# Order of the score products, the place of the norms' variance, and the order of a key copy in an attention and mixture-of-experts kernel

## The chip, the cores and the metric

The kernel runs on one core of a Trainium2 chip. The metric is the device time of one execution in microseconds. Three executions of the kernel before took 4326.62, 4331.74 and 4331.98 us, a median of 4331.74. One more execution was profiled: 4321.7 us, of which the profile's span covers 4319.9.

## The reference, cut to what matters

The input is `x`, float32, 2 images of 128 channels by 256 x 256 pixels. One layer is computed:

- A layer norm over the channels of each pixel, then three 1x1 convolutions to q, k, v (128 channels each, 4 heads of 32).
- Attention in windows of 8 x 8 queries over 12 x 12 keys around them, with relative position logits and a fixed mask. The mask leaves to each query only the keys at an even distance in both directions, so that the pixels fall into 4 independent planes (even or odd row, even or odd column). In one plane a window has 4 x 4 queries and 6 x 6 keys.
- The softmax, the product with v, an output convolution, and a residual sum.
- A layer norm over the channels of each pixel again, a router with 8 experts of which the best 2 are kept, 8 expert matrices of 128 x 128, the gated sum and a second residual sum.

```python
x = x + conv_attention(ln_c(x), W_qkv, W_out, rel_height, rel_width)
t = to_tokens(x)
t = t + moe(ln_t(t), router_w, router_b, expert_w, expert_b)   # softmax, top 2 of 8
```

## The kernel before, in words

**Tiling.** An image is cut into strips of 8 rows (`R = 8`), 32 per image and 64 in all. A strip has 4 planes, so that there are 256 planes, numbered `n`; `i, pl = divmod(n, 4)` gives strip and plane. The main loop makes one turn for each `n`, and 7 more to finish. One turn holds, woven together, the attention of plane `n`, the projections of plane `n + 1`, the norms of a row pair, the routing of an earlier row pair, and the 8 expert products of a still earlier one.

**What a plane's attention does.** A plane of a strip has 4 rows of 128 columns: 512 queries in 32 windows of 16. The windows are taken in pairs, so that 60 keys (6 rows by 10 columns, padded to `SLOT = 64`) serve 32 queries. There are 16 pairs. `kcol` (4 buffers) holds the keys column by column: in a pair's 64 places, the row is the inner index (stride 1) and the column the outer one (stride 6). Scores stand in PSUM transposed: keys on the partitions, queries along the free axis. 8 pairs use partitions 0 to 63 of the tile `att` (`half` 0), the other 8 partitions 64 to 127 (`half` 1), and each head has a PSUM bank of its own.

- `scores` (line 462) first puts the position logits into `att` (line 474, 16 products with 128 queries each), then adds the products of keys and queries (line 491). These are 64 products: for each `t` of 8, each `half` of 2 and each head `h` of 4, one with 32 rows (the channels of a head, on partitions 32 h to 32 h + 31), 64 columns (the keys) and 32 queries. The row group that a product uses in TensorE's array is set by the head, the column half by `half`. The trace shows two matmul and two weight-load records for each float32 product, 128 of each for line 491 in a plane. An exponential on ScalarE follows (line 499).
- `attend` (line 503) sums the weights over the keys (line 512) and multiplies with v (line 522): again 64 products, with 64 rows (a half), 32 columns (a head) and 32 queries. VectorE then forms `o` (lines 532 to 542), and `out_project` multiplies with the output matrix (line 550) and adds the residual (line 555).
- `project` (line 400) makes the next plane's v rows (line 350), position projections (409), keys (423) and queries (445). The new keys go from PSUM into `kcol` with two ScalarE copies for each run of rows: line 434 for the 14 inner pairs, line 441 for the two at the ends. A run has 4 rows in two of every three strips, and two runs of 2 rows stand in the third.

**Norms.** `norms` (line 563) makes the statistics of two row pairs in one tile `plt` on TensorE (line 580), and VectorE transposes them into `plg`, a PSUM tile of 512 columns of which the first 128 are used (line 589). `rstd` (line 222) takes mean and mean square from `plg` and computes variance, plus epsilon, and its inverse root, on 4 to 8 columns: copy (232), square (233), variance (234), floor and epsilon (235) on VectorE, logarithm and exponential on ScalarE (236, 237), a Newton step on VectorE (238, 239, 596, 598). The tiles `u` (variance) and `r` are in SBUF, and so is `epsc`, the table of the two epsilons. `route` and `spread` use the result in the next turn.

**What sets the order.** The main loop runs under a manual schedule: every engine executes its instructions in the order in which the loop issues them. The engines meet only at semaphores. VectorE makes 6 of the 8 gated inputs of the experts (line 705), GpSimd the other 2; GpSimd is held back by a small copy (`last`, line 709) until VectorE has made its last one, then multiplies one, makes a row of `xn` (line 276), in one turn of four copies a halo row (line 250), and multiplies the second. SyncE's queue issues all DMAs of the loop in order. Before the scores of each plane from `n = 6` on, line 823 (`addr_align`) puts fillers into TensorE's instruction stream, so that it lies at a fixed place in a block of 256 instructions; the trace shows 31 NOP records in each steady turn, right after TensorE's wait for `o` and over 2.2 us.

## Time and profile before

| | |
|---|---|
| median of three executions | 4331.74 us |
| profiled execution: time, span | 4321.7 us, 4319.9 us |
| TensorE matmul, busy | 4217.3 us, 98% of the span |
| TensorE weight load, busy | 2466.8 us, 57% |
| VectorE, busy | 3852.5 us, 89% |
| ScalarE, busy | 1452.8 us, 34% |
| GpSimd, busy | 1086.0 us, 25% |
| granted TensorE clock, mean | 0.992 |
| DMA: mean rate | 237 GB/s |

A row of a profile gives an engine, a line of the kernel, the operation, output and inputs with partitions by elements, and a count; in lists of groups the busy time and the mean of one follow, and the idle time just before them with what ended it. In lists in order of time the first column is the start in us, the second the time taken. Matmul records overlap: a busy TensorE is not a TensorE at its peak, so that the time of a stage is read from start to start. Where a wait is put down to "issue", the engine waited for nothing that the profile shows.

### The profile page before, as it was taken

To read this page: it belongs to the slowest core of one execution; us is meant where nothing else is said; L and a number is where in the kernel's file an instruction comes from. 1 tells how busy PE (TensorE), PEld (TensorE's weight loads), DVE (VectorE), ACT (ScalarE), POOL (GpSimd) and SP (SyncE) were. 2 spreads that over 40 slices of the span, in tenths; PEclk is the share of its full clock that TensorE was granted. 3 is DMA by queue.
4 is the path that set the end of the run, shared out by engine and by line. 5 is a ranking of instruction groups with operands and counts; after the bars stand their busy time and mean duration, and the time that the engine had idled before them with its cause. 6 is when DMAs were issued, how large, how long until landed. Compare 5 with 4: busy or idle time off the path is not lost. (4 is left out here: it accounts for less than half of the span.)

```text
span 4319.9 us, 224653 instructions
## 1 busy us (share of the span) xinstructions
PE 4217.3 (98%) x94273; PEld 2466.8 (57%) x94273; DVE 3852.5 (89%) x11850; ACT 1452.8 (34%) x3774; POOL 1086.0 (25%) x1126
## 2 busy tenths in 40 slices
PE   7899999999999999999999999999999999999987
PEld 4455555555555555555555555555555555555553
DVE  4799999999999999999999999999999999999977
ACT  3333333333333333333333333333333333333321
POOL 1222222222222222222222222222222222222211
PEclk9999999999999999999999999999999999999999
DMA  3678777787777777778787777777778787877765
GB/s 109 209 236 247 240 247 242 241 246 242 245 242 244 247 240 248 243 239 247 241 248 240 246 243 243 245 242 246 241 243 244 240 250 238 247 247 241 243 193 191
DMA packets 824580, 1022.19 MB, mean 237 GB/s; under 512 B 137634, under 2 KB 409634, under 8 KB 823594
## 3 DMA queue, kind: packets, MB, share of 16 engines
q1 hardware_dynamic: 822864, 1007.52, 75.4%
q8 instruction: 769, 12.60, 1.3%
q14 instruction: 217, 1.78, 0.1%
q10 hardware_dynamic: 730, 0.29, 0.0%
HBM read 863.78 MB, written 143.75 MB: 233 GB/s over the span
## 5 line engine op out<-in xcount | busy, mean ns | idle before, releaser
L714 PE MATMUL acc<-xe,ew 128*128 128x512 f32 x4096 | 1915.4, 600 | 18.6 <-DVE gb L688 16.5
L714 PEld LDWEIGHTS acc<-xe,ew 128*128 128x128 f32 x4096 | 758.1, 190 | 936.6 <-issue 886.5
L705 DVE TENSOR_TENSOR xe<-xs,gb 128x512 f32<-128x512 f32 x1536 | 950.6, 686 | 11.1 <-DMA gb<-gd 1.1
L709 POOL COPY last<-xe 128x1 f32<-128x1 f32 x256 | 47.1, 184 | 3113.7 <-DVE gb L688 3107.2
L705 POOL TENSOR_TENSOR xe<-xs,gb 128x512 f32<-128x512 f32 x512 | 650.6, 1272 | 1.5 <-PE att L522 0.7
L491 PE MATMUL att<-qs,kcol 32*64 32x32 f32 x32768 | 400.6, 226 | 11.1 <-issue 10.8
L434 ACT COPY kcol<-pk 128x560 f32<-128x560 f32 (+2 forms) x344 | 318.8, 927 | 275.3 <-PE pk L423 272.5
L491 PEld LDWEIGHTS att<-qs,kcol 32*64 32x64 f32 x32768 | 396.7, 131 | 13.9 <-issue 13.6
L276 POOL TENSOR_TENSOR xn<-xt,rb 128x512 f32<-128x512 f32 x249 | 373.7, 1501 | 91.1 <-DMA rb<-gd 74.6
L522 PEld LDWEIGHTS att<-pT,vwin 64*32 64x32 f32 x32768 | 348.6, 105 | 40.8 <-issue 3.2
L522 PE MATMUL att<-pT,vwin 64*32 64x32 f32 x32768 | 345.1, 200 | 2.4 <-issue 2.2
L499 ACT ACTIVATE pT<-att 128x1024 f32<-128x1024 f32 x256 | 261.9, 1023 | 180.3 <-PE att L491 180.1
L350 PE MATMUL pv<-wt,xn 128*128 128x128 f32 x2048 | 301.1, 291 | 0.9 <-issue 0.9
L574 ACT ACTIVATE sq<-xt 128x512 f32<-128x512 f32 x505 | 291.8, 629 | 0.0
L397 DVE STREAM_TRANSPOSE au<-auT 128x512 f32<-128x512 f32 x256 | 272.1, 1063 | 9.0
L550 PE MATMUL po<-o,wt 128*128 128x512 f32 x512 | 264.9, 599 | 9.5 <-DVE o L542 5.9
L409 PE MATMUL pu<-xn,wrel 128*128 128x512 f32 x512 | 266.2, 602 | 1.2 <-issue 1.2
L445 PE MATMUL pq<-xn,wt 128*128 128x512 f32 x512 | 261.9, 592 | 0.9 <-issue 0.8
L423 PE MATMUL pk<-xn,wt 128*128 128x512 f32 (+2 forms) x528 | 261.4, 578 | 0.0
L350 PEld LDWEIGHTS pv<-wt,xn 128*128 128x128 f32 x2048 | 251.7, 193 | 11.8 <-issue 1.3
L474 PEld LDWEIGHTS att<-au,keys 32*64 32x64 f32 x8192 | 118.9, 132 | 234.0 <-PE po L550 181.1
L413 DVE STREAM_TRANSPOSE uT<-pu 128x512 f32<-128x512 f32 x256 | 177.1, 692 | 65.5 <-PE pu L409 63.6
(2696 smaller groups left out, 4946.0 us busy)
## 6 DMA issues: line engine op xcount, KB each, us to landing
gb<-gd SPq DMA_DIRECT2D x2048, 256.0 KB, 5.5
vwin<-vrows SPq DMA_DIRECT2D x512, 240.0 KB, 5.1
xt<-in_x_dram SPq DMA_DIRECT2D x256, 256.0 KB, 6.5
sb<-gd SPq DMA_DIRECT2D x256, 256.0 KB, 4.1
out_dram<-xt SPq DMA_DIRECT2D x256, 256.0 KB, 6.0
rb<-gd SPq DMA_DIRECT2D x249, 256.0 KB, 3.4
vrows<-vr SPq DMA_DIRECT2D x168, 256.0 KB, 3.8
vrows<-vr SPq DMA_DIRECT2D x160, 128.0 KB, 3.3
```

The costliest lines, as they stand in the source:

```text
L276: eng.tensor_tensor(xn[i % 2][:, :, :, k, 1 : PC + 1], ln1_src(i, k).rearrange("p (y j x) -> p y x j", y=2, x=2), rb.rearrange("p (y j x) ...
L350: nc.tensor.matmul(pv[:, j * P : (j + 1) * P], lhsT=xp[:, k, 1 : PC + 1], rhs=wv, start=True, stop=True,)
L397: nc.vector.transpose(au.rearrange("p m a s -> p a s m"), auT[n % 2])
L409: nc.tensor.matmul(pu, lhsT=wrel, rhs=inner, start=True, stop=True)
L434: nc.scalar.copy(places[:, 1 : NP - 1], windows(new[:, :, KC - 3 :], 0, NP - 2))
L445: nc.tensor.matmul(pq, lhsT=wq, rhs=inner, start=True, stop=True)
L491: nc.tensor.matmul(sc[rows, h, 32 * t : 32 * t + 32], lhsT=kk[hp, half * HP + t, :], rhs=qs[hp, m0 : m0 + 2].rearrange("p m a s -> p (m a ...
L522: nc.tensor.matmul(av[hp, half, 32 * t : 32 * t + 32], lhsT=vv[rows, t, hp], rhs=pT[rows, h, 32 * t : 32 * t + 32], start=True, stop=True,)
L550: nc.tensor.matmul(po, lhsT=wo, rhs=state["o"].rearrange("p f z -> p (f z)"), start=True, stop=True)
L574: nc.scalar.activation(sq, src, AF.Square)
L705: eng.tensor_tensor(self.xe[e], self.xs, self.gb.pop(e), ALU.mult)
L714: nc.tensor.matmul(self.acc, lhsT=ew[:, e, :], rhs=self.xe.pop(e), start=(e == 0), stop=not self.xe)
```

## The change

Three edits, in three functions.

- In `scores`, the loops over `half` and `h` are exchanged: two products that follow each other now share the head (and so the row group and the PSUM bank) and differ in the column half, where before they shared the column half and differed in the head.
- In `rstd`, the variance `u` is no tile in SBUF any more. It stands in PSUM, in the 8 columns of `plg` behind the 128 that are used (`norms` hands them over). The square of the mean goes into a new small SBUF tile `m`. The number and order of instructions on every engine stay. The last operand rows of lines 234, 235, 238, 239, 596, 598 and of the logarithm now name `plg` where they named `u`, and the first Newton instruction waits on ScalarE alone, where it waited on ScalarE and VectorE.
- In `project`, the copy of line 434 runs through the same elements in another order: the row of a run is now the inner index (in `kcol` stride 1, in PSUM stride 128) and the column the next one; before, the column was the inner one (in `kcol` stride 6, in PSUM stride 1).

No DMA, no GpSimd instruction and no wait of TensorE or SyncE is added, removed or moved.

```diff
-    def rstd(p4, k0, k1, name):
-        u, r = (
-            small.tile([P, 2, NT], F32, tag=v, name=f"{v}_{name}")[:, k0:k1] for v in ("u", "r")
+    def rstd(p4, room, k0, k1, name):
+        u = room.rearrange("p (k t) -> p k t", t=NT)[:, k0:k1]
+        r, m = (
+            small.tile([P, 2, NT], F32, tag=v, name=f"{v}_{name}")[:, k0:k1] for v in ("r", "m")
         )
...
         nc.vector.tensor_copy(r, mean)
-        nc.vector.tensor_tensor(u, r, mean, ALU.mult)
-        nc.vector.scalar_tensor_tensor(u, u, -1.0, sq, ALU.mult, ALU.add)
+        nc.vector.tensor_tensor(m, r, mean, ALU.mult)
+        nc.vector.scalar_tensor_tensor(u, m, -1.0, sq, ALU.mult, ALU.add)
         nc.vector.scalar_tensor_tensor(u, u, 0.0, epsc[:, k0:k1], ALU.max, ALU.add)
...
-                nc.scalar.copy(places[:, 1 : NP - 1], windows(new[:, :, KC - 3 :], 0, NP - 2))
+                nc.scalar.copy(
+                    places[:, 1 : NP - 1].rearrange("p t r c -> p t c r"),
+                    windows(new[:, :, KC - 3 :], 0, NP - 2).rearrange("p t r c -> p t c r"),
+                )
...
-            for half in range(2):
-                rows = slice(half * SLOT, (half + 1) * SLOT)
-                m0 = 2 * (half * HP + t)
-                for h in range(HEADS):
-                    hp = slice(h * DH, (h + 1) * DH)
+            for h in range(HEADS):
+                hp = slice(h * DH, (h + 1) * DH)
+                for half in range(2):
+                    rows = slice(half * SLOT, (half + 1) * SLOT)
+                    m0 = 2 * (half * HP + t)
                     nc.tensor.matmul(
                         sc[rows, h, 32 * t : 32 * t + 32],
                         lhsT=kk[hp, half * HP + t, :],
...
-        r, u = rstd(p4, k0, k1, nm)
+        r, u = rstd(p4, plg[:, P : P + 2 * NT], k0, k1, nm)
```

## The prediction

> **What bounds the kernel now.** I read the page first, then one turn (one plane, `n`) in order of time for each engine, then the same rows over the whole run.

> ```profile
> PE 4217.3 (98%) x94273; PEld 2466.8 (57%) x94273; DVE 3852.5 (89%) x11850; ACT 1452.8 (34%) x3774; POOL 1086.0 (25%) x1126
> ...
> L491 PE MATMUL att<-qs,kcol 32*64 32x32 f32 x32768 | 400.6, 226 | 11.1 <-issue 10.8
> L434 ACT COPY kcol<-pk 128x560 f32<-128x560 f32 (+2 forms) x344 | 318.8, 927 | 275.3 <-PE pk L423 272.5
> L522 PE MATMUL att<-pT,vwin 64*32 64x32 f32 x32768 | 345.1, 200 | 2.4 <-issue 2.2
> ```

> TensorE is 98% busy, VectorE 89%. To see which of them sets a turn, here is TensorE in one turn, from line 474 of one plane to that of the next:

> ```profile
> 2033.08 0.69 PE L474 MATMUL att<-au,keys 32*64 32x128 f32 x32
> 2033.57 1.53 PE L491 MATMUL att<-qs,kcol 32*64 32x32 f32 x128
> 2035.03 1.16 PE L350 MATMUL pv<-wt,xn 128*128 128x128 f32 x8
> ...
> 2042.59 1.34 PE L522 MATMUL att<-pT,vwin 64*32 64x32 f32 x128
> 2043.86 0.43 PE L580 MATMUL plt<-xt,rw 128*32 128x128 f32 x8
> ...
> 2048.40 1.02 PE L714 MATMUL acc<-xe,ew 128*128 128x512 f32 x2
> 2049.36 0.47 PE L474 MATMUL att<-au,keys 32*64 32x128 f32 x16
> ```

> The turn is 2049.36 - 2033.08 = 16.28 us, and no row of it shows a wait: stage follows stage. Start to start, the score products (L491) take 1.46 us, the value products (L522), as many, 1.27. The 236 turns from plane 10 on take 16.39 us in the mean, 141 of them under 16.30 with a median of 16.27.

> VectorE and GpSimd at the end of a turn:

> ```profile
> 2013.62 0.69 DVE L542 TENSOR_TENSOR o<-att,rT 128x512 f32<-128x512 f32 x1
> 2014.26 1.26 POOL L705 TENSOR_TENSOR xe<-xs,gb 128x512 f32<-128x512 f32 x1
> ...
> 2014.99 0.16 DVE L234 SCALAR_TENSOR_TENSOR u__120_38453<-u__120_38453,plg 128x8 f32<-128x8 f32 x1
> 2015.19 0.36 DVE L235 SCALAR_TENSOR_TENSOR u__120_38453<-u__120_38453,epsc 128x8 f32<-128x8 f32 x1
> 2015.76 1.02 PE L714 MATMUL acc<-xe,ew 128*128 128x512 f32 x2
> ...
> 2016.06 0.17 DVE L238 SCALAR_TENSOR_TENSOR u__120_38453<-u__120_38453,r__120_38454 128x8 f32<-128x8 f32 x1 [0.52 <-ACT r__120_38454 L237]
> 2016.82 0.70 PE L474 MATMUL att<-au,keys 32*64 32x128 f32 x32
> ```

> L234 and L235 are the same operation on the same 8 columns, 0.16 and 0.36 us. L235 ends (2015.55) when GpSimd's product ends (2015.52): both its inputs are in SBUF, those of L234 are not, so it is held until GpSimd has finished. Over the run L235 takes 127.5 us for 260 instructions, L234 42.0. In three turns of four L235 takes about 0.37, in the fourth, with the halo copy on GpSimd, 0.93. Apart from this VectorE has no gap in a turn but the 0.52 us for ScalarE's logarithm and exponential. Its own cycle, from its starts against those of TensorE, is 16.12 us after an L235 of 0.36 and 16.43 after one of 0.67. With 0.93 it is about 16.69, and the mean of three short and one long is 16.26: as long as TensorE's 16.27. Two engines bound this kernel, TensorE by a hair.

> Where they meet, line 474 starts at least 2.47 us after L542 has ended (the fillers in the stream lie between), in the median 2.81. In this turn it is 2016.82 - 2014.31 = 2.51: VectorE was late, and the stretch from the last L714 to L474 is 1.06 us and not the 0.95 of the turn above. In 51 of 237 turns this stretch is longer, 40 of them the third of a strip, in all by 6.7 us. The rest of the excess (26.6 us over 236 turns) is mostly TensorE waiting inside L491, L522 or L714 for nothing that the profile shows, which no edit touches.

> **The change, part by part.**

> *Variance in PSUM.* L235 has one SBUF input left (`epsc`) and is not held: 0.36 becomes 0.16 as in L234 and 0.93 too. What writing to PSUM costs a small VectorE instruction no row shows. From below 0, as reading it costs nothing (L233 and L234 read `plg` in 162 ns, L239 reads SBUF alone in 166). From above 20 ns: the only VectorE row that writes PSUM, the transpose L589 of 128 columns, takes 326 ns, where the transposes to SBUF (L651, 64 columns, 245; L413, 512 columns, 675) give 306 for that size. Four instructions write there: 0 to 0.08 us, and I take 0.05. ScalarE's logarithm reading PSUM: 0, since its copy out of PSUM (L358, 512 columns, 0.59) is no slower than its square out of SBUF (L574, 0.63). VectorE's cycle goes from 16.12 (16.69) to 16.12 - 0.20 + 0.05 = 15.97 us in every turn, 0.3 under TensorE's. It then keeps up and waits for TensorE at L532. The gain is what VectorE's lateness costs TensorE now, 6.7 us. The norms' results reach the DMAs of `gd` and GpSimd's L276 up to 0.3 us sooner, which TensorE doesn't wait for in a steady turn: 0. No row puts a loss above that 0.08. Part: -6.7 us.

> *Key copy.* L434 takes 1.19 us for 560 columns, twice the pace of ScalarE's other copies (L447, 512 columns in runs of 4: 0.60). It will take between 0.65 (that pace) and 2.4 (twice as slow, as the read now strides in PSUM). I take 0.7, as the runs of 4 in `kcol` are those of L447. It costs nothing either way: behind it on ScalarE are L441, L447 and the two squares L574, done by 2008.28 in that turn, and TensorE needs the first square at 2011.35. If L434 took 3 us more, L580 would wait.

> *Order of the score products.* No instruction and no wait is added: 128 weight loads and matmuls as before. Does the new neighbourhood change their pace? Two rows of this trace bear on it. In L474 (same tiles, 128 queries) the 32 matmuls start in bursts of eight, 6.7 ns apart, and burst follows burst after 109 ns, about the time that 128 columns take (512 take 0.43 us in L714). So eight run side by side: four row groups times two column halves, and both halves of one row group at once. In L522 four products in a row share their rows and differ in columns only, which is what the new order does with two: there a product starts every 16.7 ns with no stall. In L491 products start every 16.7 ns too, with a pause of some 45 ns after every 17, 330 ns for 17; the two passes of one product lie 77 ns apart (L522: 50). The pauses come from how long a product with 64 columns of weights stays in flight, and each of the 8 tiles is visited once in 8 products in the old order and the new. I take 0. The lower bound is L522's pace: 1.27 - 1.46 = -0.19 us a plane, by 256 planes -49 us. The upper: the second product of a pair starts 77 ns after the first (as the two passes of one product do) and not 16.7: 32 pairs by 60 ns are 1.93 us, a quarter of it with four row groups side by side: +0.48 us a plane, +124 us. I take 0 because the rows nearest in kind (both halves at once in L474, shared rows in L522) show no price.

> [...]

> Sum: -6.7 + 0 + 0, rounded to -7 us. The profiled execution would take 4321.7 - 7 = 4314.7. It was 10 us faster than the median of the three runs, which lie 5 us apart; against that median the time is 4331.74 - 7 = 4324.7 us, 0.16% less. About 0.2% (8.7 us) is what a measurement of this kernel can tell from no change.

> **The rivals.**

> *B: alternating halves lets the score products run at L522's pace.* For it: L522 has the same count and shares rows between neighbours, and shows no pauses. Against it: its weights are 32 columns, those of L491 64, which fits the longer lag of the second pass. TensorE's turn would be 16.27 - 0.19 = 16.08, still above VectorE's 15.97, so that all of it counts: 4331.7 - 49 - 7 = 4276 us. Without the variance edit VectorE's 16.26 would have kept most of it back.

> *C, slower: the two products of a pair get into each other's way*, in the row group's weight load or in the bank that they now share. Place: L491. Price: up to +124 us, 4449 with the 7 off. It decides from 7 us / 256 = 27 ns a plane (2% of the stage) against the gain, and from 61 ns it is slower by over 0.2%. Nothing covers it, as TensorE sets the turn. Against it stand L474 and L522.

> *D: the stall moves.* VectorE has other instructions with two SBUF inputs; the next is L614, 0.89 us behind L474's start, when GpSimd has been done for 1.9 us. It comes 0.2 us sooner, 0.8 after a halo copy, and is still behind GpSimd's end. If it were held in the fourth turns, some of the 6.7 us stay: 4328 us.

> **How the numbers follow.** The sum (A, with D in it) 0.56, its own range 4318 to 4333; B, whole or in part, 0.24; C 0.20, kept that high because no row shows exactly this order. The range takes in B with its lowest price (4274) and the small end of C (4345), and leaves out about 0.16. Faster by over 0.2% (under 4323.1): B's 0.24 and two fifths of A, 0.23, as the sum lies 1.6 us from the border and runs differ by more: 0.47. Slower by over 0.2%: most of C, 0.19. Within: 0.34.

> **What would show it.** L235's successor at 0.16 to 0.18 us in every turn and no fourth turn at 0.93; the stretch from the last L714 to L474 at 0.95 us in all turns; VectorE waiting for TensorE at the `sT` transpose. L434 well under 1.19, with nothing following from it. L491 to L350 at 1.46 us: 1.27 would be B, 1.5 or more C. The prediction is wrong if that stage moves by more than 27 ns, since 256 planes multiply it.

## The result, and the profile after

The changed kernel took 4325.88 us in the median of four executions (4320.42 to 4332.40), beside 4331.86 for the kernel before (4326.62 to 4332.45, four executions). The medians differ by 6 us, 0.14%. The ratio over all executions is 0.9989, with a 95% interval from 0.9972 to 1.0007, so that the difference is not told apart from no change. A larger set (below, `a_again`: 12 executions against 29) gave 4323.18 against 4326.46, ratio 0.9994 [0.9981, 1.0006]. One kernel's executions spread over 20 us and more, so differences of 3 to 6 us in medians say little by themselves. What the edits do is read from the traces.

The profiled execution of the changed kernel took 4328.49 us, its span 4326.7. From its page, total times and groups:

```profile
PE 4223.3 (98%) x94273; PEld 2472.0 (57%) x94273; DVE 3791.0 (88%) x11850; ACT 1320.7 (31%) x3774; POOL 1087.6 (25%) x1126
...
L493 PE MATMUL att<-qs,kcol 32*64 32x32 f32 x32768 | 402.1, 227 | 15.8 <-issue 15.4
...
L524 PE MATMUL att<-pT,vwin 64*32 64x32 f32 x32768 | 346.7, 200 | 2.7 <-issue 1.5
...
L433 ACT COPY kcol<-pk 128x560 f32<-128x560 f32 (+2 forms) x344 | 183.5, 533 | 275.0 <-PE pk L422 272.2
```

VectorE is busy 61 us less and ScalarE 132 us less, and TensorE, which sets the end, is as busy as before. (Line 493 was 491, 524 was 522, 433 was 434, 476 was 474, and so on.)

VectorE, GpSimd and TensorE at the end of a turn, in order of time:

```profile
2020.76 0.69 DVE L544 TENSOR_TENSOR o<-att,rT 128x512 f32<-128x512 f32 x1
...
2021.41 1.26 POOL L707 TENSOR_TENSOR xe<-xs,gb 128x512 f32<-128x512 f32 x1
...
2022.13 0.17 DVE L233 SCALAR_TENSOR_TENSOR plg<-m__120_38454,plg 128x8 f32<-128x8 f32 x1
...
2022.34 0.17 DVE L234 SCALAR_TENSOR_TENSOR plg<-plg,epsc 128x8 f32<-128x8 f32 x1
...
2023.00 0.17 DVE L237 SCALAR_TENSOR_TENSOR plg<-plg,r__120_38453 128x8 f32<-128x8 f32 x1 [0.49 <-ACT r__120_38453 L236]
...
2023.31 1.02 PE L716 MATMUL acc<-xe,ew 128*128 128x512 f32 x2
...
2024.26 0.69 PE L476 MATMUL att<-au,keys 32*64 32x128 f32 x32
```

The floor instruction (L234, before L235) takes 0.17 us while GpSimd's product runs from 2021.41 to 2022.67: it is no longer held. The stretch from the last L716 to L476 is 0.95 us. In turns 10 to 245 it is longer than that in 2 turns, by 0.4 us in all; before, in 50 turns, by 6.7 us. Now VectorE waits for TensorE. Its lists of waits say where (total us, times, longest). Before:

```profile
DVE uT L413 <- PE pu L409: 63.6, 39, 13.9
```

After:

```profile
DVE uT L412 <- PE pu L408: 134.9, 252, 14.7
DVE sT L534 <- PE att L524: 21.6, 36, 1.7
```

That is the transpose `uT` of nearly every turn, not `sT`. So VectorE's lateness, the one thing that the prediction counted on, is gone. Where are the 6.7 us? TensorE in the order of time, a turn later:

```profile
2033.76 1.34 PE L524 MATMUL att<-pT,vwin 64*32 64x32 f32 x128
...
2039.58 1.02 PE L716 MATMUL acc<-xe,ew 128*128 128x512 f32 x2
2040.53 0.69 PE L476 MATMUL att<-au,keys 32*64 32x128 f32 x32
2041.02 0.37 PE L493 MATMUL att<-qs,kcol 32*64 32x32 f32 x17
2041.88 1.34 PE L493 MATMUL att<-qs,kcol 32*64 32x32 f32 x111 [0.50 <-issue]
2043.15 1.16 PE L349 MATMUL pv<-wt,xn 128*128 128x128 f32 x8
```

| us (number of waits) | before | after |
|---|---|---|
| stretch ahead of the position products | 6.7 (50) | 0.4 (2) |
| score products | 13.0 (29) | 21.1 (39) |
| expert products | 2.6 (9) | 5.9 (18) |
| value products | 3.6 (20) | 6.1 (39) |
| median turn | 16.273 | 16.269 |

The first row gains 6.3 us, and the three below it lose 13.9. Whether this is chance or a consequence is what the runs have to tell.

### The profile page after: what moved, and what is told of

Its sections match the earlier page's. It is cut to its first block, busy times and chain, and to the rows that moved or that the text cites. A ratio compares the mean times of both kernels' runs of the same rounds, so it can differ in the third digit from the quotient of the medians.

```text
span 4326.7 us, 224393 instructions
## 1 busy us (share of the span) xinstructions
PE 4223.3 (98%) x94273; PEld 2472.0 (57%) x94273; DVE 3791.0 (88%) x11850; ACT 1320.7 (31%) x3774; POOL 1087.6 (25%) x1126
## 5 line engine op out<-in xcount | busy, mean ns | idle before, releaser
L716 PE MATMUL acc<-xe,ew 128*128 128x512 f32 x4096 | 1917.9, 601 | 18.6 <-DVE gb L690 14.3
L716 PEld LDWEIGHTS acc<-xe,ew 128*128 128x128 f32 x4096 | 758.4, 190 | 939.7 <-issue 873.1
L433 ACT COPY kcol<-pk 128x560 f32<-128x560 f32 (+2 forms) x344 | 183.5, 533 | 275.0 <-PE pk L422 272.2
L447 PE MATMUL pq<-xn,wt 128*128 128x512 f32 x512 | 262.1, 592 | 1.7 <-issue 1.7
L349 PEld LDWEIGHTS pv<-wt,xn 128*128 128x128 f32 x2048 | 254.1, 195 | 11.5 <-issue 1.0
L476 PEld LDWEIGHTS att<-au,keys 32*64 32x64 f32 x8192 | 117.6, 132 | 228.2 <-PE po L552 183.8
```

What stands on the lines that cost most here:

```text
L349: nc.tensor.matmul(pv[:, j * P : (j + 1) * P], lhsT=xp[:, k, 1 : PC + 1], rhs=wv, start=True, stop=True,)
L447: nc.tensor.matmul(pq, lhsT=wq, rhs=inner, start=True, stop=True)
L716: nc.tensor.matmul(self.acc, lhsT=ew[:, e, :], rhs=self.xe.pop(e), start=(e == 0), stop=not self.xe)
```

## The experiments

The theory going in: all of the gain comes from VectorE being in time, because the floor instruction lost one of its two SBUF inputs; the other two edits are neutral. Rivals: another edit brings it; the place of the result counts and not the inputs; nothing reaches the end. Expectations are quoted as recorded before each run.

**One edit at a time.** `e1_norms` is the kernel before with the new `rstd` alone:

```diff
...
-        r, u = rstd(p4, k0, k1, nm)
+        r, u = rstd(p4, plg[:, P : P + 2 * NT], k0, k1, nm)
```

> The variance edit alone, on the kernel before. Theory (the whole gain comes from VectorE no longer being late for `o`): the floor instruction takes 0.17 us instead of 0.51 on the mean, the stretch from the last expert product to the position products is longer than usual in fewer than 5 of some 236 turns instead of 50 (excess under 0.7 us instead of 6.7), VectorE waits some 130 us for TensorE ahead of the transpose uT as in the changed kernel, and the time is about 6 us below the kernel before: 4326, ratio 0.9986. Score stage 1.459 us and inner key copy 1.19 us as before. Rival (order or key copy brings the gain): the excess goes, but the time stays within 1 us of the kernel before, because TensorE finds another wait.

Measured: 4330.53 us in the median of 12 (4324.94 to 4343.40) against 4329.24 for the kernel before (35 executions), ratio 1.0003 [0.9991, 1.0016]. The trace did what was expected (floor 36.92 us for 213 instructions, stretch excess 0.4 us in 3 turns, a wait of 140.4 us at `uT`), the time did not: 6 us less lies outside the interval. The waits at the three places came to 28.4, 4.2 and 9.0 us. So the gain does reach TensorE's stretch, and the run is not shorter for it. The rival's wording ("TensorE finds another wait") fits this edit itself.

`e2_order` is the kernel before with the loops exchanged alone:

```diff
-            for half in range(2):
...
-                for h in range(HEADS):
...
+            for h in range(HEADS):
...
+                for half in range(2):
...
```

> The exchange of the half and head loops alone, on the kernel before. Theory: order is neutral, since every tile of the array (head by half) is used once in eight products in both orders: score stage 1.456 us from start to start as in the changed kernel instead of 1.459, so 0.8 us in all planes; the 6.7 us of excess in the stretch ahead of the position products stay; time 4331, ratio 0.9998. Rival (order brings the gain): 4326, and the excess is smaller. Rival (two products that share a row group are in each other's way, hidden by another edit in the changed kernel): score stage over 1.48 us and a time over 4338.

Measured: 4326.78 us (4313.98 to 4337.45), ratio 0.9989 [0.9976, 1.0002]; stage 1.457 us; excess of the stretch 6.9 us in 50 turns. The order is neutral in the stage. The 3 ns that seemed to separate the orders (1.459 and 1.456) do not belong to it: `e3_keycopy` with the old order shows 1.457, and a later profile of the changed kernel 1.459.

`e3_keycopy` is the kernel before with the new copy alone:

```diff
-                nc.scalar.copy(places[:, 1 : NP - 1], windows(new[:, :, KC - 3 :], 0, NP - 2))
+                nc.scalar.copy(
+                    places[:, 1 : NP - 1].rearrange("p t r c -> p t c r"),
+                    windows(new[:, :, KC - 3 :], 0, NP - 2).rearrange("p t r c -> p t c r"),
+                )
```

> The column by column key copy alone, on the kernel before. Theory: the copy of 560 columns takes 0.65 us instead of 1.19 and ScalarE is busy 132 us less in all, but nothing waits for it: excess of 6.7 us and stage times as before, time 4332, ratio 1.0000 within 0.0008. Rival (the copy brings the gain, because the query copy that stands behind it on ScalarE comes earlier, or VectorE has less company in PSUM): 4326, ratio 0.9986.

Measured: 4328.16 us (4321.17 to 4339.73), ratio 0.9996 [0.9985, 1.0008]; stretch excess 6.7 us in 47 turns. ScalarE's groups (count, busy us, mean ns, then the idle time ahead of them), the kernel before and then this one:

```profile
L434 ACT COPY kcol<-pk 128x560 f32<-128x560 f32 x168 | 200.0, 1190 | 180.3 <-PE pk L423 180.3
L434 ACT COPY kcol<-pk 128x280 f32<-128x280 f32 x160 | 108.1, 676 | 86.1 <-PE pk L423 83.5
```

```profile
L434 ACT COPY kcol<-pk 128x560 f32<-128x560 f32 x168 | 108.4, 645 | 180.0 <-PE pk L423 180.0
L434 ACT COPY kcol<-pk 128x280 f32<-128x280 f32 x160 | 66.8, 418 | 86.3 <-PE pk L423 83.7
```

The copy of 560 columns takes 645 ns where it took 1190, that of 280 takes 418 where it took 676, and the stretch and the medians of TensorE's stages are as before.

**What held the floor instruction.** `e4_psum_input` keeps `u` in SBUF and gives the instruction another second operand, which stands in PSUM:

```diff
-        nc.vector.scalar_tensor_tensor(u, u, 0.0, epsc[:, k0:k1], ALU.max, ALU.add)
+        nc.vector.scalar_tensor_tensor(u, u, 0.0, sq, ALU.max, ALU.add)
```

> The kernel before with one operand of the floor instruction changed: it adds the mean square (`sq`, in PSUM) instead of the epsilon table (`epsc`, in SBUF). So the computation is changed: the norms get variance plus mean square where they got variance plus epsilon. The variance `u` stays in SBUF, as input and as output. Theory (two inputs in SBUF, while GpSimd works, are what holds the instruction up): 0.16 to 0.18 us on the mean, no instruction of 0.3 us or more beside GpSimd's expert product, excess under 0.7 us, time 4326, ratio 0.9986. Rival (the place of the result counts: a write to SBUF is held up, a write to PSUM not): 0.51 us on the mean as before, excess 6.7 us, time 4332.

Busy time of the floor instruction between 500 and 4000 us of the run (its column is the time in us and the count; then granted clock, DMA share, GB/s), in the kernel before, the changed kernel and `e4_psum_input`:

```profile
500.00:4000.00 3500.00, 108.66 (x214) 1.00 0.79 244
```

```profile
500.00:4000.00 3500.00, 37.09 (x213) 1.00 0.80 243
```

```profile
500.00:4000.00 3500.00, 34.45 (x213) 1.00 0.80 243
```

These are 508, 174 and 162 ns each. So the two SBUF inputs are the cause, shown with the result still in SBUF (508 ns with two, 162 with one); the place of the result is not. The last two differ in the place of the result, and 12 ns is what the small write to PSUM costs here.

The time was again not lower: 4329.07 us (4323.84 to 4343.88), ratio 1.0001 [0.9988, 1.0013], with the stretch excess at 0.8 us and the waits at the three places at 26.2, 4.0 and 5.4 us. Two ways of bringing VectorE into time, and neither shortens the run by 6 us.

**What changed for the blocks.** In the three profiles with VectorE late (before, `e2_order`, `e3_keycopy`) the waits in the expert and value stages sum to 6.2, 5.3 and 7.5 us; in the five with VectorE in time and the same blocks and broadcasts (after, `e1_norms`, `e4_psum_input`, and below `a_again` and `e7_60_columns`) to 12.0, 13.2, 9.4, 11.1 and 12.0. The groups don't overlap; the means are 6.3 and 11.5. The score stage's waits vary more (13.0 to 24.3 and 15.6 to 28.4), and their groups do overlap. SyncE's queue shows what else moved. Kernel before, the broadcasts of gate rows 4, 6 and 5 around a turn that begins (line 474) at 2033.08:

```profile
2032.26 0.32 SPq L689 DMA_DIRECT2D gb<-gd  x1
2033.47 0.32 SPq L689 DMA_DIRECT2D gb<-gd  x1
2034.57 0.32 SPq L689 DMA_DIRECT2D gb<-gd  x1
```

The changed kernel, around a turn that begins at 2024.26:

```profile
2023.07 0.32 SPq L691 DMA_DIRECT2D gb<-gd  x1
2024.30 0.32 SPq L691 DMA_DIRECT2D gb<-gd  x1
2025.40 0.32 SPq L691 DMA_DIRECT2D gb<-gd  x1
```

From the turn's begin these are -0.82, 0.39 and 1.49 us before, and -1.19, 0.04 and 1.14 after. In the median over turns 10 to 245 the three are issued some 0.4 us earlier (-0.77, 0.44 and 1.53 us before, -1.19, 0.03 and 1.14 after). Each writes 256 KB. They wait for small VectorE and ScalarE instructions (L690, L688) that stand behind the norms, and the norms are earlier now. The first block packet of a turn then lands later from the turn's begin: 4.36, 4.44 and 4.48 us in the median with VectorE late, 4.50 to 4.68 with VectorE in time. The second lands at 8.53 to 8.63 and 8.63 to 8.82. The second theory, so far only argued: TensorE's block packets stand behind gate broadcasts that now start earlier, and that gives back what the norms gained.

**The same pair with lighter DMA.** `l_before` and `l_after` send each gate row to a quarter of the partitions:

```diff
-            self.gb[e] = gates.tile([P, NT * P], F32, tag="gb", name=f"gb{nm}", bufs=8)
+            self.gb[e] = filled[len(fetched) % 8]
+            fetched.append(e)
...
-            nc.sync.dma_start(self.gb[e], to_all(self.gd, e))
+            nc.sync.dma_start(self.gb[e][0:32], to_all(self.gd, e)[0:32])
```

> The kernel before with lighter DMA: each broadcast of a gate row (`gb`) goes to 32 partitions instead of 128, into eight fixed tiles filled with 0.125 once, so that three quarters of the gates are left out and the experts' inputs are not the reference's. Everything else, the order of instructions too, is as in the kernel before. Theory (the variance edit saves its 6.7 us, but TensorE loses as much in waits for its own instruction blocks, whose fetches stand behind the gate broadcasts): the waits inside the score, value and expert stages fall from some 27 us in turns 10 to 245 to under 6, the excess of the stretch ahead of the position products stays at 6 to 7 us in about 50 turns, time 4300 (4290 to 4310). Rival (these waits have nothing to do with DMA traffic): 4330 and the waits stay.

> The changed kernel with the same lighter DMA: gate rows go to 32 partitions instead of 128, so that three quarters of the gates are left out. To be compared with the kernel before under the same lighter DMA. Theory: waits for instruction blocks under 6 us here too, stretch excess under 1 us, and now the gain shows: 6 us below the lighter kernel before (5 to 7.5; ratio of the two about 0.9986). Rival (the 6.7 us were never on the path that sets the end): the two agree within 1.5 us.

Measured, 12 executions each in the same rounds: 4329.49 us (4326.60 to 4335.18) for `l_before` and 4319.64 (4311.58 to 4325.74) for `l_after`. The ranges do not overlap; the medians are 9.85 us apart. Against the unaltered kernel before in these rounds (4324.32 us, 23 executions) the ratios are 1.0020 [1.0011, 1.0028] and 0.9992 [0.9982, 1.0003]. Waits of TensorE, `l_before`:

```profile
PE att L474 <- issue: 33.0, 13, 13.9
PE att L491 <- issue: 17.9, 36, 2.1
```

`l_after`:

```profile
PE att L476 <- issue: 31.4, 8, 13.4
PE att L493 <- issue: 19.0, 37, 1.6
```

and, for comparison, the changed kernel with its full traffic:

```profile
PE att L476 <- issue: 32.0, 8, 14.0
PE att L493 <- issue: 15.4, 30, 1.9
...
PE acc L716 <- issue: 3.0, 7, 0.7
...
PE att L524 <- issue: 1.5, 7, 0.3
```

With lighter DMA the first block packet of a turn lands at 2.87 us of the turn in the median of `l_before`, where it landed at 4.36, and the waits in the expert and value stages are gone in both (some 0.1 us by starts). Those of the score stage stay (28.5 and 29.4 us), and now the gain in the stretch stands. In turns 10 to 245 the stretch excess is 5.5 us against 0.8, and these turns are 5.8 us shorter.

Two things were expected wrongly. The score waits did not go, and the time of `l_before` is not 4300: it is above the unaltered kernel. Where the waits stayed, the DMA engines had not become free. Counted by the time within a turn at which DMA packets start, they were busy 72% of the first 10 us before and 31% in `l_before`, but 93% of the time from 11 to 16 us in both, where the block for the score stage is fetched: the remaining transfers crowd there, and the packet for that stage lands at 15.18 us of the turn in the median (14.33 before). And 9.85 us is more than the 6 that the stretch explains. The profiles (spans 4327.2 and 4319.0) put 5.8 us into turns 10 to 245 and the rest ahead of and behind them; no run explains that rest.

**VectorE's slack.** `e9_three_more` repeats the first instruction of `rstd` three times in the changed kernel:

```diff
         nc.vector.tensor_copy(r, mean)
+        nc.vector.tensor_copy(r, mean)
+        nc.vector.tensor_copy(r, mean)
+        nc.vector.tensor_copy(r, mean)
```

> The changed kernel with the copy of the mean (first instruction of `rstd`) issued four times instead of once: three VectorE instructions more in each turn, some 0.2 us each from start to start. Theory (VectorE's slack behind TensorE is 0.24 to 0.30 us a turn): the first 0.27 is covered, the other 0.3 us is not, so that a turn takes 16.6 us (16.5 to 16.7) and the time is 4405 (4380 to 4430); VectorE's wait ahead of uT is gone, and the stretch ahead of the position products is longer in most turns. Rival (VectorE has slack for more than 0.6 us a turn): 4330.

Measured: 4353.82 us in one execution; the median turn is 16.51 us. The direction held: VectorE sets the turn, and of its waits ahead of `uT` 15 are left, while TensorE waits ahead of its position products 156 times (lines here are 3 higher than in the changed kernel):

```profile
DVE uT L415 <- PE pu L411: 51.6, 15, 14.5
```

```profile
PE att L479 <- issue: 61.5, 156, 14.0
```

The size was off. Three copies, 0.20 us from start to start, are 0.60; the turn grew by 0.24, so the slack was 0.36 us and not 0.27. The mean turn grew less, from 16.41 us in `a_again` to 16.53, 29 us over 236 turns, partly because the waits at block ends became fewer (14.0 us against 26.7). The run also bears on the second theory: here the gate broadcasts come later against TensorE, the first two block packets land at 4.05 and 8.10 us, and the waits in score, expert and value stages are 10.3, 0.7 and 3.0 us, the least of the profiles with full traffic.

**Are the waits block fetches?** `e10_shift` moves TensorE's stream against the blocks:

```diff
-BLOCK, FIRST_LIMIT = 256, 99
+BLOCK, FIRST_LIMIT = 256, 131
```

> The changed kernel with FIRST_LIMIT 131 instead of 99: TensorE's instruction stream stands 32 instructions further ahead of the ends of the blocks of 256. The waits inside the score stage, put down to issue, fell at its instruction 35 of 256; those in the value stage at its matmul 106 of 128; those in the expert products at the second of eight. Theory (they are late fetches of the next block of 256 instructions, asked for when the block before it is begun): the places move by 32 instructions, to 67 of 256 in the score stage, into the sums over the keys and to matmul 122 of the value stage; the middle block then lasts 1.3 us instead of about 4, while a fetch has taken some 3.8 us from the start of the block to the first instruction, so that TensorE waits 2 to 2.5 us in nearly every turn in the value stage: 16.27 becomes 18.3 to 18.8 us, time 4850 to 4970. Rival 1 (blocks are fetched two ahead): places move, but the time is within 40 us of the changed kernel. Rival 2 (the waits have another cause): places and time as in the changed kernel.

Measured: 4333.54 us in one execution. The kernel before took 4310.98 to 4330.94 in the same rounds, and the changed kernel 4315.39 to 4335.77 in later ones. A wait in the score stage of `e10_shift`, and one of the changed kernel (profile of `a_again`):

```profile
2023.59 1.16 PE L493 MATMUL att<-qs,kcol 32*64 32x32 f32 x95 [0.51 <-issue]
```

```profile
2031.67 1.34 PE L493 MATMUL att<-qs,kcol 32*64 32x32 f32 x111 [0.62 <-issue]
```

95 matmuls are left of the stage's 128 where 111 were: the waits of this stage moved by 16 matmuls, 32 instructions, and those of the value stage by 16 too (from matmul 106 to 122). So the waits are at block ends, which is shown. The other half of the expectation fell: no 550 us. The middle block now begins among the sums over the keys, about 9.3 us into the turn, and lasts some 1.4 us, yet the value stage's waits are 8.8 us over turns 10 to 245. The second packet lands at 8.62 us in the median, as in the changed kernel (8.73), before the middle block begins. So a packet is not asked for when the block before it starts executing. The time is as rival 1 has it, but that blocks are fetched two ahead was not shown; what asks for a packet stays open.

**Moving a broadcast.** `c_late` puts the fetch of row 6, the one that came earliest against TensorE, behind the first part of the next turn's routing:

```diff
+            nxt.fetch(6, dve)
             nxt.fetch(5, nc.scalar)
...
-            new.fetch(6, dve)
```

> The changed kernel once more, unaltered, with more executions beside the kernel before. Theory (VectorE's lateness is gone, worth 6 to 10 us, but under the full gate broadcasts some 5 to 10 us of it come back as waits for instruction blocks in the value and expert stages): 3 us below the kernel before (0 to 6), ratio 0.9993. Rival (the gain stands whole): 7 us below, ratio 0.9984.

> The changed kernel with one gate broadcast moved: the fetch of gate row 6 (with its small VectorE write) stands not at the end of a turn but in the next turn, after the first part of the routing and just ahead of the fetch of row 5. Theory (in the changed kernel the broadcasts of the turn's begin are issued 0.4 us earlier than before, and the fetches of TensorE's instruction blocks stand behind them): the broadcasts of rows 6 and 5 are issued at about 1.0 and 1.5 us of a turn instead of 0.05 and 1.15, the first block fetch of a turn ends at 4.3 us or earlier instead of 4.63, the waits of the value and expert stages in turns 10 to 245 fall from 12 us to under 7, VectorE stays in time (stretch excess under 1 us), and the time is 5 us below the changed kernel in the same rounds (3 to 8). Rival (those waits came from chance): waits and time within 2 us of the changed kernel. Rival (row 6 now comes too late for VectorE's product): VectorE waits for gate row 6, turns get longer, time over 4340.

Measured in the same rounds: the changed kernel (`a_again`) 4323.18 us (4315.39 to 4335.77), ratio 0.9994 [0.9981, 1.0006]; `c_late` 4322.95 (4317.14 to 4340.51), 0.9997 [0.9984, 1.0010]; the kernel before 4326.46. Rows 6 and 5 were issued at 1.08 and 1.49 us of a turn, the first block packet landed at 4.18 us (4.50 in `a_again`), and the waits in the expert and value stages were 7.2 us where `a_again` has 11.1: that link of the second theory is borne out by an edit that moves two broadcasts and little else, in one profile of each. The other runs with the blocks at the same places stand in the same order: the first packet lands at 2.87 us with waits of some 0.1 (`l_before`), at 4.05 with 3.7 (`e9_three_more`), at 4.18 with 7.2 here, at 4.36 to 4.48 with 5.3 to 7.5 (VectorE late) and at 4.50 to 4.68 with 9.4 to 13.2. The time did not follow. The score stage's waits were 26.4 us against 15.6 in those two profiles, and by the medians of 12 the two kernels are equal. The packet for that stage lands at much the same time in both (14.44 us in `a_again` and 14.52 in the median), and no run ties the difference to this edit; from profile to profile of kernels with the same traffic these waits range from 13.0 to 28.4 us.

**Shorter weights.** `e7_60_columns` leaves the four padded keys out of the score products:

```diff
-                    rows = slice(half * SLOT, (half + 1) * SLOT)
+                    rows = slice(half * SLOT, half * SLOT + NK)
...
-                        lhsT=kk[hp, half * HP + t, :],
+                        lhsT=kk[hp, half * HP + t, 0:NK],
```

> The changed kernel with 60 instead of 64 columns of weights in the score products (`kk[hp, half * HP + t, 0:NK]`, output rows 0 to 59 of each half): the four padded keys are left out of the product; they are zero and the position products have written their places. Theory (the pace is set by the starts, 16.7 ns for each of two streams, and by a pause after 17 products): if the pause comes from products that stay in flight for 299 ns from first weights to last pass, and these get shorter by a sixteenth, 1.456 us becomes 1.43 to 1.44 a stage, 4 to 6 us in all; if starts alone count, 1.456 stays and the time is that of the changed kernel. Rival (a product that doesn't fill its tile's columns is slower): over 1.47 us and a time above the changed kernel's.

Measured: 4321.49 us (4312.83 to 4326.91), ratio to the kernel before 0.9984 [0.9974, 0.9995], the only kernel here with all of the computation whose interval lies below 1. Its group of score products, with 60 columns of weights:

```profile
L493 PE MATMUL att<-qs,kcol 32*60 32x32 f32 x32768 | 395.9, 223 | 21.0 <-issue 20.7
```

The stage takes 1.434 us in the median instead of 1.459 (`a_again`, same rounds), 25 ns by 256 planes = 6.4 us, and the median turn is 16.247 us. That fits the reading that the pauses after 17 products come from how long a product stays in flight, which no run shows apart. Against `a_again` itself the medians differ by 1.7 us and the ranges overlap, so that the step from the changed kernel is shown in the stage, not in the time.

**What a real conflict of tiles costs.** `e6_same_tile` makes `t` the innermost loop and keeps the break at half way:

```diff
-        for t in range(HP):
...
-            for h in range(HEADS):
...
-                for half in range(2):
...
+        for h in range(HEADS):
...
+            for half in range(2):
...
+                for t in range(HP):
```

> The changed kernel with `t` as the innermost loop of the score products: eight products in a row use the same head and the same half, so the same 32 by 64 tile of the array, before the next tile is used. In the kernel before and in the changed one a tile is used once in eight products. Theory (the order of half and head is neutral because the eight tiles work side by side; what counts is when a product meets its own tile again): now each product has to wait for the one ahead of it in its tile. The low pass of a product starts 77 ns behind its high pass, so at least 55 to 77 ns a product instead of 22.8: the stage takes 3.5 to 5 us instead of 1.46, turns 18.3 to 19.8 us, time 4850 to 5250. Rival (products queue in order for the whole array, whatever their tiles): 1.46 us a stage and a time within 10 us of the changed kernel.

The rival fell. Measured: 6351.73 us in one execution; the stage takes 7.47 us in the median. Within a tile, a matmul record starts 58 ns after the one ahead of it (two records a product, which the expectation calls passes; what each computes no trace shows), and eight products with the change of tile take 727 ns, 91 ns each instead of 22.8. That alone makes 5.8 us a stage, more than the 3.5 to 5 expected, whose 55 to 77 ns a product counted one record where there are two. The rest, which no theory had foreseen, is the clock. Four windows of one score stage (us, busy TensorE and count, granted clock, DMA share, GB/s):

```profile
2007.14:2009.14 2.00, 2.00 (x58) 1.00 0.78 214
2009.14:2011.14 2.00, 2.00 (x48) 1.00 0.57 181
2011.14:2013.14 2.00, 2.00 (x30) 0.53 0.02 6
2013.14:2014.74 1.60, 1.60 (x20) 0.50 0.00 0
```

About 4 us into the stage the granted clock falls to one half and stays there until 2018.1, 3.4 us behind the stage's end, so that the v rows behind it take 1.87 us instead of 0.99. The clock is at one half for 6.83 us, then at full rate for 17.07, and falls again some 4 us into the next score stage, which begins at 2031.17. By its records TensorE was busy for the whole of all four windows, with one 32 by 64 tile in use at a time. What lowers the granted clock here was not tried further.

## Why the prediction came out right, point by point

The forecast was 4324.7 us, the first result 4325.88, the larger set 4323.18: the number held. Its reason held in part, and that the first median came within 1.2 us is luck: the executions behind it spread over 12 us.

- *Variance in PSUM.* That the instruction "is held until GpSimd has finished" was right, and `e4_psum_input` shows that it is the inputs. The instruction went to 0.17 us, with none at 0.93. The price of a PSUM write was put at 0 to 20 ns and measures about 8 to 12. VectorE's margin was put at 0.3 us and measures 0.36.
- *"The gain is what VectorE's lateness costs TensorE now, 6.7 us."* The cost itself went as said, from 6.7 us to 0.4. The step that failed is the sentence behind it: the norms' results come earlier at the DMAs, "which TensorE doesn't wait for in a steady turn: 0". TensorE does not wait for those transfers, but the packets with its instructions land later when they start earlier. The gate broadcasts that hang on the norms start some 0.4 us earlier, the blocks for the expert and value stages land 0.1 to 0.2 us later in the mean of the profiles, and the waits there go from 6.3 us to 11.5. Of the 6.3 us gained in the stretch, 5.2 are lost there, which leaves some 1 us. The prediction had seen these waits and set them aside as ones "which no edit touches"; that was the mistake. `e1_norms` and `e4_psum_input` show it in the time (no gain, 6 us outside both intervals), the pair with lighter DMA shows the gain when these waits are taken away, and `c_late` shows that the place of a broadcast moves them. That the score stage's waits grow for the same reason was not shown. With them the four rows of the table sum to between 26 and 38 us in the profiles with VectorE late and between 27 and 42 with it in time, so that no gain can be read from the sums.
- *"It then keeps up and waits for TensorE at L532"* (`sT`): it keeps up, but the place was wrong. It waits at `uT`, early in the turn.
- *Key copy*: 0.7 taken, 0.65 measured, and 0 for the time, as `e3_keycopy` has it.
- *Order of the score products*: 0 taken; 1.457 us with either order. The argument, that each of the eight tiles is used once in eight products in both orders, is borne out by `e6_same_tile`, where it is not so. Two products of one row group next to each other, in different column halves (`e2_order`), took no longer than the old order (`e3_keycopy`).
- *Rivals.* B (L522's pace) and C (pairs in each other's way) fell with the stage at 1.457. D (the stall moves to the next VectorE instruction with two SBUF inputs) fell in the place it named: the stretch is longer than usual in 2 turns only. That a gain is taken back by a wait elsewhere was right in kind; the wait was on TensorE's instructions and not on VectorE's.

The measured 6 and 3 us against the kernel before are thus not evidence for the 6.7: by the stretch and the expert and value stages some 1 us is expected, and both sets allow that as well as nothing.

## What to carry to other kernels

When an engine that feeds DMA issues becomes earlier, ask what those transfers stand in front of: a wait that the profile puts down to "issue" can be for the engine's own instructions, and it is part of the sum (here 6.3 us in two stages became 11.5). Where a small instruction looks slow, compare it with its twin: two SBUF inputs beside a GpSimd product made 0.16 us into 0.36 or 0.93, and one input in PSUM ended that (0.16). For small products in tiles of the array, the order among different tiles cost nothing here (1.457 us a stage), using one tile eight times in a row cost four times the pace (91 ns a product for 22.8) and half the clock as well for 6.83 us, and leaving the padding out of the weights saved 25 ns a stage.

## What the runs showed that was not expected

- TensorE's instruction blocks of 256 cost 19 to 42 us of waits a run in turns 10 to 245 of the profiles with full traffic and VectorE not made the bound, at the three places that are block ends. These waits are larger than what the three edits were worth, and their size differs from profile to profile of one kernel (33.1 and 26.7 us in the two of the changed one), as do the times.
- Lighter DMA did not shorten the kernel before: 4329.49 against 4324.32 us, ratio 1.0020 [1.0011, 1.0028]. That the block of the score stage lands later (15.18 against 14.33 us) speaks for a cause there; it was not tried apart.
- With one tile in use at a time, TensorE was given half its clock (0.53 and 0.50 in the last two of the four windows above), although it was busy throughout the stage.
